# Graph attention from gathered neighbours: edge lists taken from 16-bit words, gathers in groups of three slots

## The chip, the cores and the metric

The kernel runs on one core of a Trainium2 chip. The metric is the device time of one execution in microseconds (us). A core has five engines that run side by side, each in its own order: PE (TensorE, matrix products and transposes), DVE (VectorE, elementwise work, reductions, the eight largest of a row), ACT (ScalarE, activation functions and copies), POOL (GpSimd, here mostly the issuer of indirect DMAs) and SP (SyncE, here only an issuer of DMAs). 16 DMA engines move data between the large memory (HBM) and the core's own memory (SBUF). PE writes to a third memory, PSUM.

## The reference

One graph layer over N = 4096 nodes, D = 512, 8 heads of 64, feed-forward width F = 2048, all in float32. `adj` is a 4096 x 4096 int32 matrix of zeros and ones with about 17 ones a row, `x` the source nodes, `h_target` the target nodes, and `nodemask` is all ones:

```python
hs = layer_norm(x); ht = layer_norm(h_target)
q = (ht @ Wq + bq) / 8; k = hs @ Wk + bk; v = hs @ Wv + bv      # per head
logits = where(adj != 0, q . k, -1e30); probs = softmax(logits)
ht = layer_norm2(ht + (probs @ v) @ Wo + bo)
out = normalise(x + ht + gelu(ht @ W1) @ W2)
```

Only about one logit in 240 is not masked, so the kernel gathers the neighbours' key and value rows rather than computing all logits.

## The kernel before, in words

**Projection (`project`).** `x` and `h_target` are taken 256 rows at a time: normalised (statistics on DVE, the power for 1/sqrt on POOL, scaling on ACT), transposed on PE, multiplied by the weights on PE. For `x` the result is a row of 512 keys and 512 values, stored to the DRAM table `kvd` (4 KB a row; row 0 is zero and serves as padding). For `h_target` it is the query next to the residual row, stored to `tq` (from POOL's queue for the first 20 tiles of 128 target rows, from SP's for the last 12).

**Edge lists (`edges`, L619).** For each tile of 128 target rows the adjacency rows are read in four quarters of 1024 columns. ACT takes the sign (bf16 zeros and ones, with the row's sum as its degree). DVE multiplies by 1 to 128, the position within a segment of 128 columns (L628), and takes the eight largest of each of the eight segments (`max`, L631). The 32 x 8 candidates of a tile get their segment's offset (L634, L637), and five rounds of eight-largest (L641) with four removals (L643) give up to 40 column numbers, row number + 1, into `R`. A count against the degree (L645, and the check in `sort`) raises a flag when a list isn't complete; a flag starts a general path that is not otherwise run.

**Sorting (`sort`, L653).** Target rows are sorted by degree, part A (20 tiles) and part B (12) separately: a one-hot of the degree, small products on PE, a scan on DVE, giving a rank (L690, L692). Then one indirect DMA a tile, issued on POOL, scatters the row's record (list, degree, row number) to its place by rank (L695). After that each sorted tile has a fixed cap of neighbours (`CAPS_A`, `CAPS_B`, from 40 down to 11; 600 slots over all tiles).

**Attention (`attention`, L891).** A slot is one neighbour for each of 128 target rows: one indirect DMA of 128 rows of 4 KB (L794), 512 KB. Slots are handled in groups of S = 4 (L818), each in one of four buffers `kv`. For a group DVE multiplies the keys by the query (L926), sums by head (L930), ACT takes the exponential (L934, or L944 for a tile's first group), and one group later DVE multiplies the values by it (L903, in `values`) and PE transposes and sums them in PSUM (L907). Behind each `values` the gathers of the group three ahead are issued (`issue(k + AHEAD)`). `finish` and the feed-forward (`feed`, L956: L971, gelu on ACT L974, L980) follow for tiles in pairs.

**The order.** Each of these is a Python generator that yields a cost after each portion. `_weave` (L395) always advances the stream with the smallest accumulated cost, each from its own starting value. There are three weaves: projection (all of `x` and the 20 tiles of part A's targets) with the lists of part A; then the rest of the projection with the first sort, the attention of the first three tiles (from 45) and three more lists (from 5); then attention, feed-forward, the remaining lists (at 1.9 times their cost) and the second sort. From the order so written, the language's scheduler makes one fixed order per engine and places the waits; it can move an instruction ahead of others on its engine where its own model finds that engine free. The time of the parts is thus set by queues that do not change at run time: an instruction that waits holds all behind it on its engine, and SP's queue carries adjacency loads, records, weights and `tq` stores one after another.

The lines that set the stages:

```python
_weave((proj, 0), (begin(), 0), (_take(att, early), 45), (_take(ed, 3 * steps), 5))
_weave((att, t0), (chain(feed(g) for g in range(len(GROUPS))), UNIT / 2 + LEAD), (other_lists(), t0))
```

Of the kernel before, what the change touches and what calls it, by code (L numbers as in the profile page):

```python
# [366 lines left out]
BF16 = mybir.dt.bfloat16  # L367

# [60 lines left out]
def adj_resnorm_kernel(  # L429
# [45 lines left out]
    SEG = N // P  # L475
    SQ = SEG // NQ
# [3 lines left out]
    for g in groups:  # L480
        i0 = GROUPS[-1][-1] + 1 if GROUPS else 0
        GROUPS.append(list(range(i0, i0 + len(g))))
    PARTS = ((0, len(CAPS_A)), (len(CAPS_A), len(CAPS_B)))
    S = 4
# [4 lines left out]
    kvd = dram.tile([N + 1, 2 * D], F32, name="kvd")  # L489
# [19 lines left out]
    with tc.tile_pool(name="keep", bufs=1) as keep:  # L509
# [14 lines left out]
        with ExitStack() as late:  # L524
            lp = late.enter_context(tc.tile_pool(name="lists", bufs=1))
            kp = late.enter_context(tc.tile_pool(name="kv", bufs=4))
# [24 lines left out]
            nc.gpsimd.iota(iota_i[:, :SEG], pattern=[[P, SEG]], base=0, channel_multiplier=0)  # L551
            segoff = lp.tile([P, SEG], F32, name="segoff")
            nc.vector.tensor_copy(segoff, iota_i[:, :SEG])
            nc.gpsimd.iota(iota_i, pattern=[[1, P]], base=1, channel_multiplier=0)
            lio = lp.tile([P, P], BF16, name="lio")
            nc.vector.tensor_copy(lio, iota_i)
            bins = lp.tile([P, NB], BF16, name="bins")
            nc.vector.tensor_scalar_add(bins, lio[:, :NB], -1.0)
# [60 lines left out]
            def edges(i):  # L619

                cand = lp.tile([P, SEG, 8], F32, name="cand", bufs=2)
                for h in range(NQ):
                    a = lp.tile([P, QW], I32, name="a", bufs=2)
                    nc.sync.dma_start(a, adj[i * P:(i + 1) * P, h * QW:(h + 1) * QW])
# [3 lines left out]
                    nc.vector.tensor_tensor(sg, sg, lio.unsqueeze(1).to_broadcast([P, SQ, P]),  # L628
                                            ALU.mult)
                    for s in range(SQ):  # L630
                        nc.vector.max(cand[:, h * SQ + s, :], sg[:, s, :])  # L631
                    yield 2.9
                gid = lp.tile([P, SEG, 8], F32, name="gid")
                nc.vector.scalar_tensor_tensor(gid, cand, 0.0,  # L634
                                               segoff.unsqueeze(2).to_broadcast([P, SEG, 8]),
                                               op0=ALU.is_gt, op1=ALU.mult)
                nc.vector.tensor_add(gid, gid, cand)  # L637
# [9 lines left out]
                yield 5.0  # L647
# [5 lines left out]
            def sort(part):  # L653
# [13 lines left out]
                oh = pool.tile([P, SQ, P], BF16, name="sg", bufs=3)  # L667
                oh = oh.rearrange("p s l -> p (s l)")[:, :NB * n].rearrange("p (b i) -> p b i", b=NB)
# [24 lines left out]
                yield 8.0  # L693
# [338 lines left out]
            NA, NBT = PARTS[0][1], PARTS[1][1]  # L1032
# [107 lines left out]
```

## Time and profile before

| | |
|---|---|
| median of 3 runs | 2069.45 us (2065.8 to 2073.72) |
| profiled execution | 2059.0 us, its span 2057.2 us |
| PE busy | 1762.0 us, 86% |
| DVE busy | 1682.1 us, 82% |
| POOL busy | 975.0 us, 47% |
| ACT busy | 747.3 us, 36% |
| DMA | 482.33 MB, 234 GB/s on average |
| gathers of key and value rows | 600 indirect DMAs, 708.7 us of POOL |

The span is the profiled stretch of the one core; the execution's time adds 1.8 us around it. An engine's busy time is a union of its instructions' spans; the instruction lines give a count, the busy time and the mean duration in ns, then the idle time of the engine ahead of them and what ended it. "A <- B" is a wait of A that B ended. Names are the program's own: `L628` is a line of the kernel, `sg<-sg,lio` what is written and read.

### The profile page before, as it was taken

The page shows a single profiled execution, that of the slowest core. Times are in us where ns is not written, and L with a number is a line of the kernel's source. Part 1 is how long each engine was busy: PE and PEld are TensorE (multiplying, and loading weights), DVE is VectorE, ACT ScalarE, POOL GpSimd, SP SyncE. Part 2 cuts the span into 40 slices and gives each one's busy share as a digit, 9 for nine tenths or more (in the row PEclk, how much of TensorE's full clock was granted, in tenths as well). Part 3 has the DMA queues.
Part 4 walks back from the last instruction along what each step waited for, and adds up shares of the span by engine and source line. Part 5 has one row for each costly group of instructions (what it writes and reads, how often), then busy time and mean ns, then how long its engine had stood idle before and what let it go on. Part 6 is the DMA issues. An engine that isn't in the chain of part 4 may idle for free. (4 is left out here: it accounts for less than half of the span.)

```text
span 2057.2 us, 21470 instructions
## 1 busy us (share of the span) xinstructions
PE 1762.0 (86%) x7282; PEld 1142.3 (56%) x7282; DVE 1682.1 (82%) x3022; ACT 747.3 (36%) x1170; POOL 975.0 (47%) x869
## 2 busy tenths in 40 slices
PE   6989888853489999899968998898887899989996
PEld 3444444322366666576646666566565666666664
DVE  5989999558899999999978878797878878887701
ACT  4655555322134543434322333232222243333310
POOL 1023332062445554455676556666655746654301
PEclk9999999986699999999989999999999999999998
DMA  8777776468778687786767777877777768765400
GB/s 275 241 238 242 242 239 213 160 240 321 265 265 282 232 296 240 258 268 224 255 203 263 257 253 240 278 242 269 264 237 249 265 231 271 262 223 198 143 11 23
DMA packets 145391, 482.33 MB, mean 234 GB/s; under 512 B 20293, under 2 KB 20857, under 8 KB 145273
## 3 DMA queue, kind: packets, MB, share of 16 engines
q0 software_dynamic: 100032, 359.45, 51.1%
q1 hardware_dynamic: 39536, 102.53, 15.6%
q10 hardware_dynamic: 5704, 18.89, 2.3%
q8 instruction: 60, 0.98, 0.2%
q14 instruction: 59, 0.48, 0.1%
HBM read 438.07 MB, written 42.73 MB: 234 GB/s over the span
## 5 line engine op out<-in xcount | busy, mean ns | idle before, releaser
L794 POOL DMA_INDIRECT kv<-kvd,rec x600 | 708.7, 1181 | 503.8 <-PE cps L907 287.3
L971 PE MATMUL pf<-h2T,w 128*128 128x256 f32 (+1 forms) x2176 | 476.2, 369 | 2.5 <-ACT h2T L887 2.5
L980 PE MATMUL po<-w,gt 128*128 128x512 f32 x1024 | 470.4, 595 | 0.0
L926 DVE TENSOR_TENSOR kv<-kv,tq 128x2048 f32<-128x2048 f32 (+3 forms) x160 | 344.0, 2151 | 138.5 <-DMA kv<-kvd,rec 120.4
L971 PEld LDWEIGHTS pf<-h2T,w 128*128 128x128 f32 x2176 | 389.3, 192 | 79.5 <-issue 32.7
L907 PE MATMUL cps<-ident,kv 128*128 128x128 f32 x2400 | 323.2, 291 | 121.6 <-DVE kv L903 121.2
L907 PEld LDWEIGHTS cps<-ident,kv 128*128 128x128 f32 x2400 | 294.5, 151 | 191.5 <-DVE kv L903 163.9
L903 DVE TENSOR_TENSOR kv<-kv,p 128x2048 f32<-128x2048 f32 (+3 forms) x160 | 342.4, 2143 | 15.6 <-ACT p L934 15.3
L930 DVE TENSOR_REDUCE lg<-kv 128x32 f32<-128x2048 f32 (+3 forms) x160 | 342.3, 2141 | 0.5
L980 PEld LDWEIGHTS po<-w,gt 128*128 128x128 f32 x1024 | 188.9, 192 | 175.9 <-issue 172.9
L631 DVE MAX8 cand<-sg 128x8 f32<-128x128 bf16 x1024 | 225.9, 276 | 0.1
L609 POOL TENSOR_TENSOR n_rs<-n_ve,mhalf 128x2 f32<-128x2 f32 (+1 forms) x66 | 53.8, 815 | 304.6 <-DVE n_ve L608 260.2
L626 ACT ACTIVATE sg<-a 128x1024 bf16<-128x1024 int32 x128 | 135.1, 1055 | 163.7 <-DVE cand L631 94.8
L974 ACT ACTIVATE gt<-pf 128x512 f32<-128x512 f32 x128 | 76.5, 597 | 253.4 <-PE pf L971 252.3
L934 ACT ACT_TABLE_LOAD x76 | 97.5, 1283 | 194.5 <-DVE lg L930 159.5
L751 PE MATMUL pq<-wk,hT 128*128 128x512 f32 x256 | 121.7, 620 | 17.3 <-ACT row L753 8.3
L751 PE MATMUL pq<-wv,hT 128*128 128x512 f32 x256 | 119.9, 612 | 17.3 <-DVE row L765 10.0
L974 ACT ACT_TABLE_LOAD x103 | 132.1, 1283 | 1.8
L864 PE MATMUL t<-wo,rb 128*128 128x512 f32 x256 | 122.1, 622 | 11.9 <-DVE rb L860 11.9
L934 ACT ACTIVATE p<-lg 128x32 f32<-128x32 f32 (+3 forms) x128 | 25.5, 199 | 276.6 <-DVE lg L930 171.6
L762 PE MATMUL pq<-wq,hT 128*128 128x512 f32 x256 | 121.2, 618 | 3.1 <-DVE row L765 2.6
L628 DVE TENSOR_TENSOR sg<-sg,lio 128x1024 bf16<-128x1024 bf16 x128 | 97.7, 767 | 0.8 <-ACT sg L626 0.8
(119 smaller groups left out, 1408.0 us busy)
## 6 DMA issues: line engine op xcount, KB each, us to landing
a<-in_adj_dram SPq DMA_DIRECT2D x128, 512.0 KB, 5.4
kvd<-row ACTq DMA_DIRECT2D x32, 512.0 KB, 5.5
tq<-row POOLq DMA_DIRECT2D x20, 512.0 KB, 6.1
kv<-kvd,rec POOLq DMA_INDIRECT x600, 5.8
xin<-in_L_gnn_h_target_dram SPq DMA_DIRECT2D x16, 512.0 KB, 4.9
w<-in_L_gnn_W_dram SPq DMA_DIRECT2D x8, 1024.0 KB, 9.6
xin<-in_x_dram SPq DMA_DIRECT2D x15, 512.0 KB, 5.0
tq<-row SPq DMA_DIRECT2D x12, 512.0 KB, 6.6
```

The source lines that it names most:

```text
L626: nc.scalar.activation(sg.rearrange("p s l -> p (s l)"), a, AF.Sign, accum_out=dpart[:, i, h:h + 1])
L631: nc.vector.max(cand[:, h * SQ + s, :], sg[:, s, :])
L751: nc.tensor.matmul(pkv, hT[:, kc, j * P:(j + 1) * P], w[:, kc, :], start=kc == 0, stop=kc == KC - 1)
L794: nc.gpsimd.indirect_dma_start(out=dst, out_offset=None, in_=table[:, :], in_offset=bass.IndirectOffsetOnAxis(ap=idx, axis=0))
L903: nc.vector.tensor_tensor(v4, v4, p[:, j0:j0 + n, :].unsqueeze(3) .to_broadcast([P, n, H, HD]), ALU.mult)
L907: nc.tensor.matmul(cps[:, c, :], kv[:, j, D + c * P:D + (c + 1) * P], ident, is_transpose=True, start=j0 + j == 0 and c == 0, stop=j0 + j ...
L926: nc.vector.tensor_tensor(kv[:, :n, :D], kv[:, :n, :D], tq[:, :D].unsqueeze(1).to_broadcast([P, n, D]), ALU.mult)
L930: nc.vector.tensor_reduce(lg[:, :n, :], kv[:, :n, :D].rearrange("p j (h d) -> p j h d", h=H), AX.X, ALU.add)
L934: nc.scalar.activation(p[:, j0:j0 + n, :], lg[:, :n, :], AF.Exp)
L971: nc.tensor.matmul(pf[:, k, :], w1[(f0 + k) // KC][:, kc, (f0 + k) % KC * P:((f0 + k) % KC + 1) * P], h2T[:, kc, :w], start=kc == 0, stop= ...
L974: nc.scalar.activation(gt, pf, AF.Gelu_apprx_tanh)
L980: nc.tensor.matmul(po[j], gt[:, k, j * P:(j + 1) * P], w2[(f0 + k) // KC][:, (f0 + k) % KC, :], start=False, stop=f0 + k == FC - 1, skip_g ...
```

## The change

1. **Lists from words.** The sign is written as bytes, and pairs of columns are read as one 16-bit word (low byte the even column). The quarter's 512 words are multiplied by 1, 3, 5, ... within a segment, so that each byte that is set becomes an odd position below 256, and the quarter is cut into 5 segments of 102 or 103 words in place of 8 of 128 columns. The eight largest words of a segment are kept: 20 x 8 candidates a tile, each with up to two columns. Two new instructions split them into low and high bytes (`dec`), giving 320 entries where there were 256; the offset, the five rounds and the four removals run over 320. The product goes to a tile of its own (`wd`). The index tables are built once, at the start, by 12 index fills on POOL through one buffer and 16 copies on DVE (before: 2 and 3).
2. **Groups.** S goes from 4 to 3, the `kv` buffers from four to five.
3. **Order.** In the second weave attention starts at 55 (45) and two lists (three) at 60 (5); the remaining ten lists (nine) are in the third. A list's costs in the weave are 4 x 2.0 + 6.0 (4 x 2.9 + 5.0), and the sort's portion ahead of the scatters is given 20.0 (8.0).
4. **Small parts.** The sort's one-hot has a tile of its own instead of one of `sg`'s buffers; the table `kvd` has N + 128 rows, of which the gathers see N + 1 as before.

```diff
-    SEG = N // P
-    SQ = SEG // NQ
+    WQ = QW // 2
+    SQ = 5
+    SEGS = [(s * WQ // SQ, (s + 1) * WQ // SQ) for s in range(SQ)]
+    SEG = NQ * SQ
...
-    S = 4
+    S = 3
...
-    kvd = dram.tile([N + 1, 2 * D], F32, name="kvd")
+    kvd = dram.tile([N + P, 2 * D], F32, name="kvd")
...
-            kp = late.enter_context(tc.tile_pool(name="kv", bufs=4))
+            kp = late.enter_context(tc.tile_pool(name="kv", bufs=5))
...
+            segoff = lp.tile([P, 2, NQ, SQ], F32, name="segoff")
+            for b in range(2):
+                for s, (w0, _) in enumerate(SEGS):
+                    nc.gpsimd.iota(iota_i[:, :NQ], pattern=[[QW, NQ]], base=2 * w0 + b,
+                                   channel_multiplier=0)
+                    nc.vector.tensor_copy(segoff[:, b, :, s], iota_i[:, :NQ])
...
+            nc.gpsimd.iota(iota_i, pattern=[[2, P]], base=1, channel_multiplier=0)
+            lio = lp.tile([P, WQ], U16, name="lio")
+            for w0, w1 in SEGS:
+                nc.vector.tensor_copy(lio[:, w0:w1], iota_i[:, :w1 - w0])
...
-                cand = lp.tile([P, SEG, 8], F32, name="cand", bufs=2)
+                cand = lp.tile([P, SEG, 8], U16, name="cand", bufs=2)
                 for h in range(NQ):
                     a = lp.tile([P, QW], I32, name="a", bufs=2)
                     nc.sync.dma_start(a, adj[i * P:(i + 1) * P, h * QW:(h + 1) * QW])
-                    sg = lp.tile([P, SQ, P], BF16, name="sg", bufs=3)
-                    nc.scalar.activation(sg.rearrange("p s l -> p (s l)"), a, AF.Sign,
-                                         accum_out=dpart[:, i, h:h + 1])
-                    nc.vector.tensor_tensor(sg, sg, lio.unsqueeze(1).to_broadcast([P, SQ, P]),
-                                            ALU.mult)
-                    for s in range(SQ):
-                        nc.vector.max(cand[:, h * SQ + s, :], sg[:, s, :])
-                    yield 2.9
-                gid = lp.tile([P, SEG, 8], F32, name="gid")
-                nc.vector.scalar_tensor_tensor(gid, cand, 0.0,
-                                               segoff.unsqueeze(2).to_broadcast([P, SEG, 8]),
+                    sg = lp.tile([P, QW], U8, name="sg", bufs=3)
+                    nc.scalar.activation(sg, a, AF.Sign, accum_out=dpart[:, i, h:h + 1])
+                    wd = lp.tile([P, WQ], U16, name="wd", bufs=2)
+                    nc.vector.tensor_tensor(wd, sg.bitcast(U16), lio, ALU.mult)
+                    for s, (w0, w1) in enumerate(SEGS):
+                        nc.vector.max(cand[:, h * SQ + s, :], wd[:, w0:w1])
+                    yield 2.0
+                dec = lp.tile([P, 2, SEG, 8], U16, name="dec")
+                nc.vector.tensor_single_scalar(dec[:, 0], cand, 255, op=ALU.bitwise_and)
+                nc.vector.tensor_single_scalar(dec[:, 1], cand, 8, op=ALU.logical_shift_right)
+                gid = lp.tile([P, 2 * SEG, 8], F32, name="gid")
...
-                nc.vector.tensor_add(gid, gid, cand)
+                nc.vector.tensor_add(gid, gid, dec)
...
-                yield 5.0
+                yield 6.0
...
-                oh = pool.tile([P, SQ, P], BF16, name="sg", bufs=3)
...
+                oh = pool.tile([P, NB * NA], BF16, name="oh")
...
-                yield 8.0
+                yield 20.0
...
-                    gather(kvs[k][:, j, :], kvd, recs[i][:, j0 + j:j0 + j + 1])
+                    gather(kvs[k][:, j, :], kvd[0:N + 1, :], recs[i][:, j0 + j:j0 + j + 1])
...
-            _weave((proj, 0), (begin(), 0), (_take(att, early), 45), (_take(ed, 3 * steps), 5))
+            _weave((proj, 0), (begin(), 0), (_take(att, early), 55), (_take(ed, 2 * steps), 60))
```

More of the change, by code (lines that the diff above doesn't have):

```diff
@@ L367 @@
 BF16 = mybir.dt.bfloat16
+U8 = mybir.dt.uint8
+U16 = mybir.dt.uint16
 CAPS_A = (40, 24, 23, 22, 21, 20, 20, 19, 18, 18, 17, 17, 16, 16, 15, 15, 14, 13, 12, 11)
@@ L550, in adj_resnorm_kernel @@
             iota_i = lp.tile([P, P], I32, name="iota_i")
[L551 to L556, printed above, removed]
+            segoff = lp.tile([P, 2, NQ, SQ], F32, name="segoff")
[8 more added lines that the diff above has]
+                nc.vector.tensor_copy(lio[:, w0:w1], iota_i[:, :w1 - w0])
+            nc.gpsimd.iota(iota_i, pattern=[[1, P]], base=0, channel_multiplier=0)
             bins = lp.tile([P, NB], BF16, name="bins")
-            nc.vector.tensor_scalar_add(bins, lio[:, :NB], -1.0)
+            nc.vector.tensor_copy(bins, iota_i[:, :NB])
             lower = lp.tile([P, P], BF16, name="lower")
@@ L1031, in adj_resnorm_kernel @@
             ed = all_edges()
-            NA, NBT = PARTS[0][1], PARTS[1][1]
             steps = NQ + 1
```

7 lines of the change are left out of this document (6 added, 1 removed).

## The prediction

> **What bounds the kernel now.** I read the busy totals first, then busy time by stage, because no engine is the limit throughout. The columns of the second view are the stretch, its length, and busy us (with instructions) of PE, PE's weight loads, DVE, ACT and POOL, then granted clock, DMA share, GB/s.
>
> ```profile
> PE 1762.0 (86%) x7282; PEld 1142.3 (56%) x7282; DVE 1682.1 (82%) x3022; ACT 747.3 (36%) x1170; POOL 975.0 (47%) x869
> ```
> ```profile
> 20.00:380.00 360.00, 325.30 (x872) 149.19 (x871) 327.00 (x1252) 207.01 (x377) 84.60 (x87) 0.98 0.71 229
> 453.00:487.50 34.50, 15.29 (x33) 6.62 (x32) 22.53 (x78) 10.24 (x18) 13.83 (x13) 0.75 1.00 378
> 487.50:575.00 87.50, 39.86 (x219) 33.02 (x220) 75.23 (x82) 10.88 (x25) 35.02 (x32) 0.69 0.76 277
> ...
> 380.00:575.00 195.00, 103.05 (x375) 61.60 (x374) 138.56 (x272) 42.38 (x83) 80.09 (x75) 0.75 0.73 266
> 575.00:1000.00 425.00, 398.75 (x1792) 278.05 (x1792) 414.52 (x760) 176.66 (x261) 227.75 (x196) 0.98 0.75 256
> 1000.00:1110.00 110.00, 88.77 (x401) 62.52 (x400) 90.61 (x89) 27.96 (x41) 77.85 (x65) 0.91 0.72 237
> 1110.00:1930.00 820.00, 734.77 (x3358) 515.00 (x3357) 682.55 (x580) 270.71 (x372) 488.90 (x419) 0.97 0.74 249
> 1930.00:2057.00 127.00, 107.44 (x480) 73.44 (x478) 24.05 (x51) 16.60 (x30) 11.41 (x13) 0.94 0.06 18
> ```
>
> Five stages are seen. In projection with lists (20 to 380) PE and DVE are both at about 90%. Then comes a valley (380 to 575): PE works 103 of 195 us, and in its middle the DMA share is 1.00. From 575 to 1000 attention, feed-forward and the late lists run together, and DVE, 97.5% busy, is the limit. From 1110 to 1930 there are no lists; PE has 90%, DVE 83%, and the two wait for each other and for gathers. The tail is PE's alone. So list work costs time in the first three stages and nothing after 1000.
>
> **Lists.** Instructions on DVE overlap slightly, so I price them from start to start.
>
> ```profile
> 340.72 1.28 DVE L628 TENSOR_TENSOR sg<-sg,lio 128x1024 bf16<-128x1024 bf16 x2
> 341.91 3.19 DVE L631 MAX8 cand<-sg 128x8 f32<-128x128 bf16 x16
> 345.13 0.47 DVE L634 SCALAR_TENSOR_TENSOR gid<-cand,segoff 128x256 f32<-128x256 f32 x1
> ...
> 346.67 0.40 DVE L641 MAX8 R<-gid 128x8 int32<-128x256 f32 x1
> 347.00 0.27 DVE L631 MAX8 cand<-sg 128x8 f32<-128x128 bf16 x1
> ```
> ```profile
> L631 DVE MAX8 cand<-sg 128x8 f32<-128x128 bf16 x1024 | 225.9, 276 | 0.1
> L641 DVE MAX8 R<-gid 128x8 int32<-128x256 f32 x160 | 65.8, 411 | 0.1
> L643 DVE MATCH_REPLACE8 gid<-R,gid 128x256 f32<-128x256 f32 x128 | 52.1, 407 | 0.0
> ```
>
> A product takes (341.91-340.72)/2 = 0.60 us, a segment maximum 3.22/16 = 0.20, a 256-wide maximum 347.00-346.67 = 0.33. The maxima of 128 and 256 differ by 135 ns, so 1.05 ns an element and some 0.065 us fixed. A tile before: 4 x (0.60 + 8 x 0.20) = 8.8, then eleven 256-wide instructions at 0.33 (two for the column numbers, five maxima, four replacements) with about 0.45 for value loads and the count: 4.1. Sum 12.9 us. After: five maxima of about 102 words a quarter at 0.20 - 0.027 = 0.173, and a product of 512 words. No row has a product on words: if its streaming halves it is 0.065 + 0.535/2 = 0.33, if words lose the bf16 rate it stays at 0.60. I take 0.33, since the row nearest to it is of the same two bytes an element. That is 4 x 1.20 = 4.8. The eleven become 320 wide, 0.40 each: 4.4, plus 0.45. Two decodes of 160 words are new: between 0.11 (a quarter of the streaming, 0.065 + 0.042) and 0.23 (all of it, 0.065 + 0.168); I take the middle, 0.17 each. Sum 10.0 us, at worst 4 x (0.60 + 5 x 0.20) + 5.3 = 11.7. **A tile saves 2.9 us** (1.2 at worst): 93 us of DVE over 32 tiles, 58 of them in the first stage. The sign conversion keeps its 1024 elements on ACT; byte output has no row, so I keep its price (ends: 0.2 us either way, hidden while ACT has 207 of 360 us). The product no longer writes over sg, so ACT gets its buffer back after the product, not after eight maxima.
>
> The index tables are ten more round trips between POOL and DVE at the start, ahead of the first norm on POOL:
>
> ```profile
> 11.13 0.23 POOL L554 IOTA iota_i<- 128x128 int32 x1 [8.19 <-DVE cols L574]
> ...
> 11.40 0.29 DVE L556 CAST lio<-iota_i 128x128 bf16<-128x128 int32 x1 [0.26 <-POOL iota_i L554]
> ...
> 16.54 1.01 ACT L741 ACTIVATE hT<-pt,cols 128x256 f32<-128x256 f32 x2
> ...
> 24.43 3.60 PE L751 MATMUL pq<-wk,hT 128*128 128x512 f32 x8
> ```
>
> One trip is 11.69 - 11.13 = 0.56 us, ten 5.6. The first transposed input is ready at 17.55 and used at 24.43, so 6.9 us hide them: cost 0, or 5.6 without that cover.
>
> The Trainium skill, "VectorE: DVE Perf Modes", section on the perf-mode tier table, says that a two-input elementwise instruction on 16-bit data reaches two elements a cycle and no more; the 0.60 us for 1024 elements agrees, and by that rule the product on words, also two bytes wide, would be at the lower of my two ends; at the upper one the lists of the first stage would keep 80 x 0.27 = 22 us more of DVE.
>
> *First stage.* DVE falls to 327 - 58 = 269 of 360 us, and PE's 325 remain. If PE reaches the 93.8% it has from 575 to 1000, the stage is 347 long (gain 13); at 97%, 335 (gain 25). I take **18**, ends 0 (PE held by ACT evictions) and 30.
>
> **The valley.** Next I read it in order of time, with the waits.
>
> ```profile
> 409.38 1.08 POOL L695 DMA_INDIRECT rec<-R,ranki  x1 [36.30 <-DVE ranki L692]
> ...
> 434.41 0.96 POOL L695 DMA_INDIRECT rec<-R,ranki  x1 [0.30 <-issue]
> 435.40 0.73 POOL L609 TENSOR_TENSOR n_rs<-n_ve,mhalf 128x2 f32<-128x2 f32 x1
> ...
> 440.56 1.15 POOL L794 DMA_INDIRECT kv<-kvd,rec  x1 [0.31 <-issue]
> ```
> ```profile
> 469.99 0.69 DVE L765 SCALAR_TENSOR_TENSOR row<-pq,bq 128x512 f32<-128x512 f32 x1 [11.20 <-DMA tq<-row]
> ...
> 487.52 2.27 DVE L926 TENSOR_TENSOR kv<-kv,tq 128x2048 f32<-128x2048 f32 x1
> ```
> ```profile
> 387.44 0.33 ACTq L755 DMA_DIRECT2D kvd<-row  x1
> ```
> ```profile
> kvd<-row ACTq DMA_DIRECT2D x32, 512.0 KB, 5.5
> ```
> ```profile
> 438.94 0.33 SPq L624 DMA_DIRECT2D a<-in_adj_dram  x1
> ...
> 484.92 0.33 SPq L624 DMA_DIRECT2D a<-in_adj_dram  x1
> ```
>
> Sorting, 20 scatters (409 to 435), a norm stuck behind them, first gather at 440.6, yet attention's first DVE instruction only at 487.5: the DMA engines are full, and DVE waits 11.2 us for a row buffer whose store shares SP's queue with adjacency loads. The change starts lists after attention here (60 against 5) and takes two, not three. Between the two quoted loads there are nine, 512 KB each: 4.7 MB, at 378 GB/s 12.5 us. The first four groups are 3, 3, 3 and 2 slots, against 4, 4, 3 and 4: 2.1 MB less, 5.5 us. Together 18. Further, lists cost 14.0 units in the weave, not 16.6: 20 end at 280 of the projection's 336 units (32 portions at 7.8, 20 at 4.3), so DVE is free to sort while PE projects. The gathers need the last k/v store, issued at 387.4 and landing some 5.5 us on, so at most they start at 393, 47 us earlier; at least none, if the planner leaves sorting where it is. I take 15. Against it: two lists (20 us) now lie beside attention, in a stretch where DVE has 12 us idle (75 of 87.5 busy) and which held the end of the third list: a cost of 0 to 8, and I take 3. **Valley: 30**, ends 0 and 62. The weave's new price of 20 behind the sort, on whose result POOL waits 36.3 us, puts more projection ahead of the scatters in the queues; what waits behind them is that norm and the gathers, and I count nothing.
>
> **Late lists.** From 575 to 1000 nine tiles cost 9 x 12.9 = 116 us of DVE; ten will cost 100. The finer groups give back 4 (below). With DVE at 97.5% that is **10**, ends 0 and 20. The second sort's stretch (1000 to 1110) has PE at 81% where the next has 90%, 10 us; its 12 scatters stay, so **3**, ends 0 and 10.
>
> **Groups of three, five buffers.** Summed over the tiles' caps, 160 groups become 210.
>
> ```profile
> L926 DVE TENSOR_TENSOR kv<-kv,tq 128x2048 f32<-128x2048 f32 x139 | 317.6, 2285 | 133.7 <-DMA kv<-kvd,rec 115.6 <-issue 7.5 <-DMA rec<-R,ranki 5.5
> ...
> L926 DVE TENSOR_TENSOR kv<-kv,tq 128x512 f32<-128x512 f32 x6 | 4.1, 682 | 1.2 <-DMA kv<-kvd,rec 1.2
> ```
> ```profile
> POOL kv L794 <- PE cps L907: 110.6, 33, 9.6
> ...
> DVE kv L926 <- DMA kv<-kvd,rec: 91.5, 47, 5.6
> ...
> PE cps L907 <- DVE kv L903: 54.1, 31, 6.8
> ```
>
> The second view is of 1110 to 1930. A slot costs 0.535 us and an instruction 0.14, of which some 0.08 overlaps. Fifty groups with three instructions each: 150 x 0.06 to 0.14 = 9 to 21 us of DVE, mostly where DVE has idle time; its price if it had none is the 21. The gathers stay 600. Before, a gather for group k+3 took the buffer of group k-1 and so waited for PE's transposes of the group just done; with five it takes that of k-2. But the ring holds 15 slots, not 16: less two groups in work, 9 slots are ahead instead of 8. So the 91.5 us of DVE waiting shrink a little, not wholly. At PE's 93.8% the stretch would be 783 us (gain 37); the loss end is the 21 us above. Nearest is no change: **5**.
>
> Sum: 18 + 30 + 10 + 3 + 5 = 66 us off the profiled execution's 2059.0 us (span 2057.2 and 1.8 around it): 1993. The median of the runs is 10.5 us above it, so 2069.45 - 66 = **2003 us**.
>
> **Rivals.** (1) *The ring of five works in full.* For it: 47 of 95 groups wait for a gather. Against: one slot more ahead is little. The 37 us of the long stretch, and half of what the valley has left above my value (32): 2003 - 37 - 16 = 1950.
> (2) *The valley does not move, and words lose the bf16 rate.* For it: sorting and scatters run one after another whatever DVE has free. Then the first stage gives 8, the late lists 4 (ten tiles at 11.7), the valley 8 (half of what the DMA engines are relieved of), the ring its 5: 2069 - 25 = 2044.
> (3) *Slower: exponentials come too late.* ACT changes tables between exponential and gelu:
>
> ```profile
> L934 ACT ACT_TABLE_LOAD x76 | 97.5, 1283 | 194.5 <-DVE lg L930 159.5 <-DVE n_ve L608 8.7 <-DVE degs L838 7.9
> ```
> ```profile
> 1509.07 1.28 ACT L974 ACT_TABLE_LOAD   x1
> ...
> 1510.36 0.60 ACT L974 ACTIVATE gt<-pf 128x512 f32<-128x512 f32 x1
> ```
> ```profile
> DVE kv L903 <- ACT p L934: 15.3, 17, 3.9
> ```
> A group's exponential is hidden by DVE's product and reduction of the next: 2 x 2.2 = 4.4 us with four slots, 2 x 1.67 = 3.3 with three. Behind a gelu it takes 0.6 + 1.28 + 0.2 = 2.1 us, and 3.4 when the gelu's load is still ahead too. So 1.1 us of cover go. It decides from 66/210 = 0.31 us a group; if half of the 210 wait the full 1.1, it costs 115 us: 2118. Against it: today only 17 waits, 15.3 us (the last row, of the long stretch).
>
> The Trainium skill, "ScalarE: Activation LUTs", section "What ACT_TABLE_LOAD costs", adds a drain of 1.38 us to each switch, 2.66 in all. By that the exponential behind a gelu would take 3.5 us, above the new cover, and rival (3) would be likely. The trace has the gelu 10 ns after its load's end, with no such drain, so I leave its chance low.
>
> **Chances.** Forecast 0.56, (1) 0.20, (2) 0.15, (3) 0.09. Half a percent, 10 us, is what a measurement can tell from no change. (2) may end within it (a third of its chance). So faster 0.86, same 0.05, slower 0.09. The range goes from 1935, below rival (1) by the rest of the valley's upper end, to 2060, which takes in nearly all of (2).
>
> **What would show it.** Right: segment maxima near 0.17 us from start to start, 640 of them, products near 0.33; DVE under 80% in the first stage, with PE above 92%; attention's first product before 455 us; POOL's wait for PE's transposes mostly gone, with DVE's wait for gathers still above 60 us in the long stretch. Wrong: scatters still starting 35 us after the last list (valley step), a word product above 0.5 us (list price), or DVE's third instruction waiting for exponentials by more than 60 us (rival 3).

## The result and the profile after

The changed kernel takes **2002.35 us** (median; 1995.04 to 2006.56) against 2068.22 us for the kernel before beside it: a ratio of 0.9674, 95% interval 0.9638 to 0.9710. The forecast was 2003 us. The total is right; the terms it was summed from are not, and most of this text is about that. The traces are single executions: the traced one of the kernel before took 2059.0 us, 9 us less than its median, and the traced one here 2004.54, 2 us more than its median. So the traces show 54 us between the kernels where the medians show 66.

The busy totals of the changed kernel, and its busy time by stage, with the columns as in the prediction (stretch, length, PE, weight loads, DVE, ACT, POOL, granted clock, DMA share, GB/s). The bounds are those of the prediction's stages, moved to where the same work is done now.

```profile
PE 1751.0 (87%) x7282; PEld 1133.6 (57%) x7282; DVE 1599.0 (80%) x2865; ACT 774.0 (39%) x1236; POOL 959.0 (48%) x879
```
```profile
20.00:361.00 341.00, 319.81 (x873) 148.54 (x872) 271.73 (x1052) 205.78 (x378) 83.77 (x87) 0.98 0.72 242
361.00:549.00 188.00, 108.36 (x430) 66.49 (x429) 123.58 (x220) 42.87 (x83) 84.61 (x76) 0.78 0.75 267
549.00:972.00 423.00, 405.31 (x1788) 278.53 (x1788) 409.85 (x757) 191.14 (x287) 233.66 (x203) 0.96 0.76 263
972.00:1070.00 98.00, 79.29 (x347) 54.89 (x346) 75.44 (x78) 28.80 (x44) 59.14 (x55) 0.88 0.72 247
1070.00:1879.00 809.00, 732.66 (x3398) 514.53 (x3396) 692.06 (x680) 283.34 (x409) 480.63 (x421) 0.97 0.75 254
```

DVE lost 83 us of work (1682.1 before) and left the first stage, where it has 272 of 341 us. The stages after it have nearly the shape they had.

**The list step** shows in its group by line (busy us and mean ns) and in a stretch of DVE's timeline (start, duration):

```profile
L644 DVE MAX8 cand<-wd 128x8 uint16<-128x102 uint16 (+1 forms) x640 | 130.8, 251 | 0.8
```
```profile
461.35 0.74 DVE L642 TENSOR_TENSOR wd<-sg,lio 128x512 uint16<-128x512 uint16 x2
462.01 1.76 DVE L644 MAX8 cand<-wd 128x8 uint16<-128x102 uint16 x10
463.69 1.21 DVE L944 TENSOR_TENSOR kv<-kv,tq 128x1024 f32<-128x1024 f32 x1
```

A word product takes (462.01 - 461.35)/2 = 0.33 us from start to start, a segment maximum 1.68/10 = 0.168, and there are 640 of them, as forecast.

**The valley** in order of time. Rows of several engines are put together.

```profile
309.97 1.16 DVE L687 TENSOR_TENSOR oh<-b,bins 128x960 bf16<-128x960 bf16 x1
...
372.37 0.37 PE L697 MATMUL t<-oh,ones_bf 128*128 128x480 bf16 x1
...
390.42 1.31 POOL L713 DMA_INDIRECT rec<-R,ranki  x1 [38.20 <-DVE ranki L710]
...
423.13 0.97 POOL L812 DMA_INDIRECT kv<-kvd,rec  x1 [0.30 <-issue]
...
437.17 1.76 DVE L944 TENSOR_TENSOR kv<-kv,tq 128x1536 f32<-128x1536 f32 x1 [4.84 <-DMA kv<-kvd,rec]
```

DVE has the sort's one-hot table ready at 311.1, but PE's first product on it runs at 372.37: it stands 61 us behind projection products in PE's queue (before: 17 us, from 374.97 to 391.79). The scatters start at 390.42, 19.0 us earlier than before (409.38). From the first gather to attention's first product it now takes 437.17 - 423.13 = 14.0 us, where it took 487.52 - 440.56 = 47.0. So the first product comes 50 us earlier. Then this follows on SP's queue, DVE and ACT:

```profile
473.00 6.65 SPq L1071 DMA_DIRECT2D w<-in_L_gnn_W_dram  x1
479.76 8.72 SPq L637 DMA_DIRECT2D a<-in_adj_dram  x2
497.72 1.06 ACT L640 ACTIVATE sg<-a 128x1024 uint8<-128x1024 int32 x1 [22.55 <-DMA a<-in_adj_dram]
...
498.89 1.56 SPq L637 DMA_DIRECT2D a<-in_adj_dram  x2
...
502.35 0.20 ACT L952 ACTIVATE p<-lg 128x24 f32<-128x24 f32 x1
502.59 1.75 DVE L921 TENSOR_TENSOR kv<-kv,p 128x1536 f32<-128x1536 f32 x1 [19.72 <-ACT p L952]
```

The next adjacency load goes out only at 479.76, behind six weight loads whose issue has SP from 459.39 to 479.65. Two loads are issued by 488.48; the next two follow at 498.89, when the first sign has set its load's buffer free (there are two). ACT waits 22.55 us with that sign for the first load; the exponential is queued behind the signs, and DVE waits 19.72 us for the exponential.

How far attention is can be read by counting PE's transposes (four to a slot) up to a time. The first rows are of the kernel before, the second of the changed one (columns: stretch, length, PE and weight-load busy us with counts, clock, DMA share, GB/s).

```profile
0.00:602.00 602.00, 27.27 (x162) 24.56 (x162) 0.90 0.72 244
0.00:1025.00 1025.00, 110.71 (x799) 100.80 (x800) 0.93 0.74 250
0.00:1126.00 1126.00, 133.40 (x964) 121.47 (x964) 0.93 0.73 248
0.00:1948.00 1948.00, 322.57 (x2396) 294.14 (x2397) 0.95 0.73 246
```
```profile
0.00:576.00 576.00, 26.31 (x160) 22.80 (x161) 0.91 0.73 252
0.00:997.00 997.00, 111.67 (x796) 98.62 (x797) 0.93 0.74 256
0.00:1085.00 1085.00, 131.99 (x959) 116.92 (x960) 0.93 0.75 258
0.00:1897.00 1897.00, 319.64 (x2395) 285.84 (x2396) 0.95 0.74 253
```

The same count is reached 26, 28, 41 and 51 us earlier, and the span ends 54.4 us earlier (2002.8 for 2057.2). By stage, with a second trace beside it: run B below turned out to have the same instructions in the same order on every engine.

| stage | forecast | trace | run B's trace |
|---|---|---|---|
| first stage (start of the scatters) | 18 | 19 | 7 |
| valley, to slot 40 | 30 | 7 | 8 |
| late lists, slots 40 to 200 | 10 | 2 | 6 |
| second sort, slots 200 to 240 | 3 | 13 | 12 |
| long stretch, slots 240 to 600 | 5 | 10 | 7 |
| tail | 0 | 3 | 3 |

So the first stage's gain differs by 12 us between two executions of the same instructions, and that of the late lists by 4. Smaller differences than these, between single traces, say nothing.

Whole-span waits of the changed kernel (total us, times, longest):

```profile
POOL kv L812 <- PE cps L925: 250.1, 94, 16.1
...
DVE kv L944 <- DMA kv<-kvd,rec: 118.1, 48, 7.1
...
DVE kv L921 <- ACT p L952: 33.0, 13, 19.7
```

### The profile page after: what moved, and what is told of

It reads as the page before. It is cut to its first block, busy times and chain, and to the rows that moved or that the text cites. A ratio compares the mean times of both kernels' runs of the same rounds, so it can differ in the third digit from the quotient of the medians.

```text
span 2002.8 us, 21520 instructions
## 1 busy us (share of the span) xinstructions
PE 1751.0 (87%) x7282; PEld 1133.6 (57%) x7282; DVE 1599.0 (80%) x2865; ACT 774.0 (39%) x1236; POOL 959.0 (48%) x879
## 5 line engine op out<-in xcount | busy, mean ns | idle before, releaser
L812 POOL DMA_INDIRECT kv<-kvd,rec x600 | 687.6, 1146 | 464.6 <-PE cps L925 250.1
L989 PE MATMUL pf<-h2T,w 128*128 128x256 f32 (+1 forms) x2176 | 485.9, 374 | 3.6 <-ACT h2T L905 3.6
L944 DVE TENSOR_TENSOR kv<-kv,tq 128x1536 f32<-128x1536 f32 (+2 forms) x210 | 351.2, 1674 | 130.5 <-DMA kv<-kvd,rec 118.1
L925 PEld LDWEIGHTS cps<-ident,kv 128*128 128x128 f32 x2400 | 286.4, 147 | 169.3 <-DVE kv L921 127.3
L921 DVE TENSOR_TENSOR kv<-kv,p 128x1536 f32<-128x1536 f32 (+2 forms) x210 | 349.3, 1666 | 33.2 <-ACT p L952 33.0
L948 DVE TENSOR_REDUCE lg<-kv 128x24 f32<-128x1536 f32 (+2 forms) x210 | 349.3, 1666 | 0.5
L640 ACT ACTIVATE sg<-a 128x1024 uint8<-128x1024 int32 x128 | 135.0, 1055 | 146.5 <-DMA a<-in_adj_dram 90.4
L952 ACT ACTIVATE p<-lg 128x24 f32<-128x24 f32 (+2 forms) x178 | 34.3, 193 | 320.3 <-DVE lg L948 161.4
L644 DVE MAX8 cand<-wd 128x8 uint16<-128x102 uint16 (+1 forms) x640 | 130.8, 251 | 0.8
L780 PEld LDWEIGHTS pq<-wq,hT 128*128 128x128 f32 x256 | 51.0, 206 | 78.8 <-issue 60.1
```

Of the source, the lines that this page charges most:

```text
L780: nc.tensor.matmul(pq, hT[:, kc, j * P:(j + 1) * P], wq[:, kc, :], start=kc == 0, stop=kc == KC - 1)
L812: nc.gpsimd.indirect_dma_start(out=dst, out_offset=None, in_=table[:, :], in_offset=bass.IndirectOffsetOnAxis(ap=idx, axis=0))
L921: nc.vector.tensor_tensor(v4, v4, p[:, j0:j0 + n, :].unsqueeze(3) .to_broadcast([P, n, H, HD]), ALU.mult)
L925: nc.tensor.matmul(cps[:, c, :], kv[:, j, D + c * P:D + (c + 1) * P], ident, is_transpose=True, start=j0 + j == 0 and c == 0, stop=j0 + j ...
L944: nc.vector.tensor_tensor(kv[:, :n, :D], kv[:, :n, :D], tq[:, :D].unsqueeze(1).to_broadcast([P, n, D]), ALU.mult)
L948: nc.vector.tensor_reduce(lg[:, :n, :], kv[:, :n, :D].rearrange("p j (h d) -> p j h d", h=H), AX.X, ALU.add)
```

## The experiments

All times are medians of five rounds or more beside the kernel before, which had 2069.82 us in the first four runs, 2071.75 in the next four and 2071.24 in the last four. Ratios are to that.

### The parts one by one

**Words alone.** The new lists, with their costs in the weave and the small parts, but neither groups nor order:

```diff
 changed kernel
-    S = 3
+    S = 4
-    tile_pool(name="kv", bufs=5)
+    tile_pool(name="kv", bufs=4)
-    (_take(att, early), 55), (_take(ed, 2 * steps), 60)
+    (_take(att, early), 45), (_take(ed, 3 * steps), 5)
-    yield 20.0      (after the sort)
+    yield 8.0
```


> The word lists alone (with their new weave costs of 14.0 units a tile), groups of four in four buffers, the order of before. Theory A, the prediction's steps: the first stage gives 18 us, the valley about 5 (three lists there are 2.9 us cheaper each), the late lists, DVE-bound at 97.5%, nine times 2.9 us = 26 of which some 20 are seen: 2068 - 43 = about 2025. Theory B, as the two traces line up by milestones (the stretch with late lists took as long after as before): only the first stage pays, 2068 - 19 = about 2049. In both a product on 512 words takes 0.33 us from start to start.

2033.28 us, ratio 0.9827 (0.9788 to 0.9866): 36 us, between the two theories (43 and 19). DVE's busy total falls from 1682.1 to 1600.1 us, 82 us where the list price said 93. But the gain does not lie where it was forecast. This trace reaches slot 40 at 574 us, 28 before the kernel before, slot 200 at 1010, only 15 before it, and slot 240 at 1103, 23 before it. The stretch of the late lists grew from 423 to 436 us, though DVE had 391.79 us of work in it in place of 411.10. So less list work did not shorten that stretch by itself; what held it there is not settled.

**Groups alone.**

```diff
 kernel before
-    S = 4
+    S = 3
-    tile_pool(name="kv", bufs=4)
+    tile_pool(name="kv", bufs=5)
```


> The kernel before with groups of three in five buffers and nothing else. Theory A (prediction): about 5 us faster, 2063, with DVE's wait for gathers a little shorter. Rival, the ring of five works in full: 2040 or below, POOL's and DVE's waits for buffers and gathers mostly gone. Rival, exponentials too late: slower than 2078, with DVE's third instruction waiting for ACT far above 15 us.

2003.10 us, ratio 0.9677 (0.9643 to 0.9710): 67 us, as much as the whole change, where the prediction had 5, and well past the 2040 of the rival. Counts of transposes in this run:

```profile
0.00:590.00 590.00, 25.01 (x157) 21.33 (x157) 0.92 0.73 247
0.00:1113.00 1113.00, 133.00 (x964) 116.35 (x964) 0.94 0.74 251
0.00:1528.00 1528.00, 235.52 (x1761) 207.89 (x1762) 0.95 0.76 258
0.00:1909.00 1909.00, 315.70 (x2400) 282.05 (x2400) 0.95 0.74 252
```

The kernel before reaches the first two counts at 602 and 1126, the third at 1577 and the last at 1948:

```profile
0.00:1577.00 1577.00, 240.98 (x1757) 218.36 (x1757) 0.94 0.74 250
```

So the groups win 12 us before slot 40, nothing more to slot 240, then 36 us in a stretch of 200 slots without any list work, and give 10 of these back to slot 600: the long stretch gains 26. The span ends 50.5 us earlier (2006.7 for 2057.2); the rest of the 67 is the distance of the two traced executions from their medians.

**Order alone.**

```diff
 kernel before
-    (_take(att, early), 45), (_take(ed, 3 * steps), 5)
+    (_take(att, early), 55), (_take(ed, 2 * steps), 60)
-    yield 8.0      (after the sort)
+    yield 20.0
```


> The kernel before with the new order alone: attention from 55, two lists from 60, the sort's portion at 20. Theory A (prediction's valley step): attention's first product some 20 to 35 us earlier, the valley 15 us shorter, a tenth late list of 12.9 us given back: about 2065. Theory B (order is what moves the valley, the late stage hides the tenth list): 2040.

2074.43 us, ratio 1.0025 (1.0004 to 1.0047): no gain, against both theories (2065 and 2040), and a loss too small to tell from no change. Attention does start earlier, as theory A asked: its first product runs at 466.80, 21 us before the kernel before's, and 15.8 us behind the first gather (47.0 before). But slot 40 comes at 602, no earlier than before, after a stall like that of the changed kernel: DVE waits 16.74 us for one exponential.

**Words and order without the groups.**

```diff
 changed kernel
-    S = 3
+    S = 4
-    tile_pool(name="kv", bufs=5)
+    tile_pool(name="kv", bufs=4)
```


> The changed kernel with groups of four in four buffers again. Theory A (groups are worth 5 us): 2007. Theory B (from the milestones: from the second sort on the changed kernel gained another 10 to 20 us, by the finer ring): 2020.

2048.89 us, ratio 0.9896 (0.9857 to 0.9935), slower than both theories: without the groups 47 us of the changed kernel's gain are gone. Against words alone the order costs 16 us. This trace has the same stall, 20.0 us at the longest, where words alone has 2.1.

**Words and groups in the old order.**

```diff
 changed kernel
-    (_take(att, early), 55), (_take(ed, 2 * steps), 60)
+    (_take(att, early), 45), (_take(ed, 3 * steps), 5)
-    yield 20.0      (after the sort)
+    yield 8.0
```


> The changed kernel with the old order: word lists in 20 segments, groups of 3 and five buffers, but attention from 45, three lists from 5 and a sort portion of 8. Theory A (the parts add up: groups alone took 66 us off, words alone 36): 2069 - 66 - 36 = 1967 us. Theory B (groups and words take away waits of the same stretch, so that the second of them finds little left): within 10 us of the groups alone and of the whole change, 1995 to 2010 us. Theory C (the new order is worth some 15 us once the words are there, as between the words alone at 2033 and words with order, which came out at 2049, it was not): then this kernel would be below the whole change by about 15 us, 1987 us.

1977.08 us, ratio 0.9540 (0.9514 to 0.9566). Words (36) and groups (67) nearly add up: 95 of 103 us. The new order takes 25 of them back in the changed kernel.

### What of the order costs

Three edits make the order. Two runs put one back each; a third moves the remaining lists.

```diff
 changed kernel, run A: the lists' place
-    (_take(ed, 2 * steps), 60)
+    (_take(ed, 3 * steps), 5)
```


> The changed kernel with three lists from 5 as before, in place of two from 60; attention from 55 and the sort's portion of 20 stay. Against the changed kernel (2002 us) and words with groups in the old order (1977 us). Theory A (the list that is moved out of the stretch before 500 us, where DVE is mostly idle, into the stretch that DVE fills is what the new order costs): 1977 to 1987 us. Theory B (the place of the first attention portions or of the sort is): 1997 us or more.

```diff
 changed kernel, run B: the sort's portion
-    yield 20.0
+    yield 8.0
```


> The changed kernel with the portion behind the sort back at 8 in place of 20; lists and attention stay in the new order. Theory A (the 20 pushes scatters and gathers behind more projection and later pushes the second sort behind more attention): 1977 to 1990 us. Theory B (the portion matters little): 1998 to 2006 us.

```diff
 changed kernel, run C: the lists after the sort
-    (other_lists(), t0)
+    (other_lists(), t0 + 20)
```


> The changed kernel with the remaining lists' work woven in 20 us of planned time later, behind the loads of the last weights. It tests the stretch at 482 to 502 us, in which DVE waited 19.7 us for an exponential that stood behind a sign on ACT, and that sign for an adjacency load behind weight loads on SP. Theory A (a stall of that kind sets the end by its length): 2002 - 18 = 1984 us. Theory B (the stall is moved to another place or made good by the long stretch, in which the buffers run ahead again): 1998 to 2006 us. Theory C (the lists that come later push the second sort late, and the second half's gathers with it): 2010 us or more.

A takes 1975.46 us (ratio 0.9552, 0.9522 to 0.9582), the same as the whole old order; B takes 2005.98 (0.9687, 0.9660 to 0.9715), C 1999.25 (0.9660, 0.9632 to 0.9687), both the same as the changed kernel. So it is the lists' place alone. The other two edits hardly reach the chip: the fixed order that the scheduler makes for B is that of the changed kernel, instruction for instruction on every engine, and that for A differs from the whole old order in some twenty places out of 12,500 instructions. B is thus a second measurement of the changed kernel, 4 us from the first, and no test of the portion of 20 beyond this: it changes nothing. C was meant to take the 20 us stall away and didn't: its longest wait of that kind is still 20.0 us, so the theories on the stall were not told apart by it.

A tells more. SP's queue behind the late weights, and the counts of transposes in run A:

```profile
478.93 2.50 SPq L1071 DMA_DIRECT2D w<-in_L_gnn_W_dram  x1
543.73 14.75 SPq L637 DMA_DIRECT2D a<-in_adj_dram  x4
```
```profile
0.00:571.00 571.00, 25.88 (x163) 22.70 (x164) 0.93 0.75 258
0.00:982.00 982.00, 108.10 (x800) 96.17 (x801) 0.94 0.76 261
0.00:1076.00 1076.00, 128.41 (x964) 114.85 (x964) 0.95 0.75 259
0.00:1868.00 1868.00, 311.87 (x2400) 280.65 (x2400) 0.96 0.75 257
```

With three lists from 5, the adjacency loads are out before the weights, the next come at 543.73, and no exponential stands behind a sign that waits for them: the longest wait is 2.9 us. All five kernels with the lists' new place have a wait of 16.7 to 20.0 us there, and none with the old place has one above 3.9. Run A is 5 us ahead of the changed kernel at slot 40, 15 at slot 200, 9 at slot 240, 29 at slot 600. The first 15 have two likely places: the stall, which uses up the early start of attention, and one list tile of about 10 us that the changed kernel leaves to the stretch in which DVE is 97% busy (409.85 of 423 us). The second sort gives 6 back, and 20 arise after slot 240, where no list work is left in either kernel. There the changed kernel's DVE waits more for gathers (34.8 us against 18.3 from 1150 to 1500); why the lists' place reaches so far is not settled by these runs.

### Why the groups gain

**Four buffers of three.**

```diff
 kernel before
-    S = 4
+    S = 3
```


> The kernel before with groups of 3 slots, still four buffers and gathers three groups ahead. Theory A (what the groups brought is the fifth buffer: a gather asked three groups ahead goes into a buffer set free one group earlier, so POOL no longer waits for the transposes of the group just before): with four buffers the wait is back and 12 slots are in flight in place of 16, so 2065 to 2090 us. Theory B (what they brought is the smaller group: shorter bursts of transposes and products, so that DVE and PE wait shorter for each other): 2003 to 2025 us, as with five buffers.

2115.28 us, ratio 1.0220 (1.0191 to 1.0248), slower than both theories allowed. Smaller groups alone lose 44 us; the fifth buffer turns that into a gain of 67. What a fifth buffer does for groups of four no run shows.

**Five buffers, all of them asked for ahead.**

```diff
 kernel before
-    S = 4
+    S = 3
-    tile_pool(name="kv", bufs=4)
+    tile_pool(name="kv", bufs=5)
-    AHEAD = 3
+    AHEAD = 4
```


> The kernel before with groups of 3, five buffers, and gathers asked four groups ahead in place of three: 15 slots in the ring, all of them asked for, and each gather again waits for the buffer of the group just before. Theory A (the slack of one buffer between asking and setting free is what brought the gain): it is gone, 2050 to 2075 us. Theory B (small groups are what brought it): 2003 us or a few us to either side. Theory C (more slots asked ahead would hide the gathers better, since DVE still waited 85 us for them with three ahead): below 1995 us.

2001.72 us, ratio 0.9658 (0.9631 to 0.9684): as with three ahead. The traces say why: between 1150 and 1500 us the first gather into a buffer starts 1.3 us on average after the buffer's last transposes here, 1.4 us with three ahead, and 1.2 in the kernel before. So a gather follows the freeing of its buffer just as closely, whatever group it was asked behind. The slack between asking and setting free, which the prediction describes, does not arise, so it is not the cause.

What is, one can follow in the timeline of the kernel before (rows of several engines together). The code takes the buffers in turn, so every fourth group has the same one. One use of a buffer, from its first gather to its next one (the rows at 1300.32, 1302.80 and 1310.87 are of the group behind it):

```profile
1290.27 0.95 POOL L794 DMA_INDIRECT kv<-kvd,rec  x1 [0.30 <-issue]
...
1295.32 0.94 POOL L794 DMA_INDIRECT kv<-kvd,rec  x1 [0.30 <-issue]
...
1300.32 0.93 POOL L794 DMA_INDIRECT kv<-kvd,rec  x1 [0.63 <-PE cps L907]
...
1302.00 2.25 DVE L926 TENSOR_TENSOR kv<-kv,tq 128x2048 f32<-128x2048 f32 x1
1302.80 2.27 POOL L794 DMA_INDIRECT kv<-kvd,rec  x1 [0.30 <-issue]
...
1310.87 2.29 DVE L926 TENSOR_TENSOR kv<-kv,tq 128x2048 f32<-128x2048 f32 x1 [4.30 <-DMA kv<-kvd,rec]
...
1319.67 2.28 DVE L903 TENSOR_TENSOR kv<-kv,p 128x2048 f32<-128x2048 f32 x1
...
1322.01 1.97 PE L907 MATMUL cps<-ident,kv 128*128 128x128 f32 x16 [0.32 <-DVE kv L903]
...
1324.60 0.94 POOL L794 DMA_INDIRECT kv<-kvd,rec  x1 [0.30 <-issue]
```

Four gathers are issued in 5.0 us, 6.7 us later the key product starts, 17.7 us later the values product of the same group (two other groups' key products stand between), then 4.3 us to the end of the transposes and 0.6 to the next use: 34.3 us in all, for four buffers 8.6 us a group. The count of key products in 350 us without lists, here for the kernel before, says 350/41 = 8.5 us a group:

```profile
1150.00:1500.00 350.00, 88.83 (x41) 0.97 0.76 256
```

That the two agree proves nothing yet: buffers that are taken in turn come round after n groups, whatever sets the pace. That the ring holds the work back shows in two waits of the next group. Its first gather (1300.32) waits for PE's transposes to set a buffer free, and its key product (1310.87) finds DVE idle for 4.30 us, until its last gather lands. Such waits of DVE are 39.5 us of these 350. With four buffers, two groups' time of a cycle is the wait for the values product, so n groups take (issue + landing + transposes + reuse) + 2 groups, and **a group takes that bracket divided by n - 2**. The same count for four buffers of 3, five of 3, and the last run below, each a trace of its own:

```profile
1150.00:1500.00 350.00, 88.45 (x52) 0.96 0.73 246
```
```profile
1150.00:1500.00 350.00, 98.31 (x58) 0.98 0.82 278
```
```profile
1150.00:1500.00 350.00, 105.57 (x89) 0.96 0.83 285
```

The bracket below is the mean over the groups that start in this stretch, taken in each trace from rows like those of the example; the waits are DVE's for gathers in these 350 us:

| buffers x slots | bracket us | rule, us a group | count, us a group | waits us | time us |
|---|---|---|---|---|---|
| 4 x 4 (before) | 17.4 | 8.7 | 8.5 | 39.5 | 2070 |
| 4 x 3 | 14.5 | 7.2 | 6.7 | 49.8 | 2115 |
| 5 x 3 | 16.1 | 5.4 | 6.0 | 24.4 | 2003 |
| 6 x 2 | 14.7 | 3.7 | 4.2 | 30.8 | 2032 |
| 7 x 2, words, old order | 17.4 | 3.5 | 3.9 | 8.0 | 1951 |

The waits fall in the order of the times, and so does the rule's time for one slot: 2.4 us with 4 x 3, then 2.2, 1.8 and 1.8, and 1.7 with 7 x 2. The bracket comes out of the same trace as the count, so the table is an account and not a forecast. With four buffers the rule gives what is seen, within half a microsecond. With more, the values product follows its key product by 2.2 to 2.7 groups in place of 2, and a group takes longer than the rule says. The rule says where the gain has its source, not its full size: from 5.4 to 6.0 us it is engines, or waits among them.

**Six buffers of two**, the same 12 slots as four of three:

```diff
 kernel before
-    S = 4
+    S = 2
-    tile_pool(name="kv", bufs=4)
+    tile_pool(name="kv", bufs=6)
-    AHEAD = 3
+    AHEAD = 5
```


> The kernel before with groups of 2 slots, six buffers and gathers five groups ahead: 12 slots in the ring, as in the run with groups of 3 in four buffers (2115 us). Theory A (ring rule: a buffer is held for its gathers' issue and landing, then for two whole groups until its values product, then for its transposes; so with n buffers a group takes (issue + landing + transposes) / (n - 2). From the traces between 1150 and 1500 us that gives 17.4 / 2 = 8.7 us for four buffers of 4, 14.5 / 2 = 7.2 for four of 3, 16.1 / 3 = 5.4 for five of 3, against 8.5, 6.7 and 6.0 seen; for six buffers of 2 it gives about 13 / 4 = 3.2 us, less than the 3.6 us that DVE needs for such a group, so the ring no longer binds): the gathers' waits nearly go, DVE gets 147 groups more with 0.06 to 0.14 us for each of three instructions, 26 to 62 us, and the time is 1990 to 2030 us. Theory B (what counts is the slots in flight: 12 are as slow as the other 12): 2100 us or more.

2032.06 us, ratio 0.9821 (0.9793 to 0.9850), 83 us below the other 12 slots and 2 us above the range that the ring rule gave. The number of slots in the ring alone is not what counts. The bracket was put at about 13 us and came to 14.7. That the gathers' waits nearly go did not come true: DVE still waits 83.1 us for them over the span (120.4 in the kernel before).

**Seven buffers of two, with words and the old order:**

```diff
 changed kernel, old order
-    S = 3
+    S = 2
-    tile_pool(name="kv", bufs=5)
+    tile_pool(name="kv", bufs=7)
-    AHEAD = 3
+    AHEAD = 5
```


> Words and groups with the old order (1977 us), but groups of 2 in seven buffers, gathers five groups ahead. Theory A (the ring rule: (about 13) / 5 = 2.6 us a group, not binding): of the 81 us that DVE waited for gathers most go, against 97 groups more, 17 to 41 us of DVE: 1955 to 1985 us. Theory B (a group's exponential has too little cover, two instructions of 1.2 us against 3.4 us behind a gelu): DVE's wait for exponentials grows by 0.3 us or more for each of 307 groups: 2050 us or more.

**1950.58 us**, ratio 0.9428 (0.9400 to 0.9456): 52 us below the changed kernel, the fastest run of this case, and 4 us below the range given. The busy totals and the waits that both theories name:

```profile
PE 1747.6 (90%) x7282; PEld 1131.5 (58%) x7282; DVE 1626.9 (83%) x3156; ACT 802.5 (41%) x1341; POOL 892.4 (46%) x879
```
```profile
DVE kv L944 <- DMA kv<-kvd,rec: 44.0, 37, 3.7
...
DVE kv L921 <- ACT p L952: 21.6, 35, 2.3
```

The wait for gathers falls to 44.0 us (118.1 in the changed kernel), and the exponentials, with still smaller groups, cost 21.6 us in 35 waits. DVE has 25.5 us more to do than with groups of 3 (1626.9 against 1601.4 in the run with words and groups), and it pays.

## Why the prediction was right, and where it was not

**The total is right by errors that cancel.** Groups are worth 67 us alone and stood at 5; valley and late lists stood at 40 and came to 9 in one trace of the changed kernel and 14 in the other; the order, which was to bring the valley's gain, costs 25. That these make 66 together is luck.

**Lists: the price was right, nearly.** Product 0.33 us, maximum 0.168, as forecast; DVE's total falls by 82 us, 2.6 us a tile, where 2.9 was forecast. Words alone give 36 us against the 31 that the prediction has for first stage, late lists and second sort, but this agreement is in part chance, since the late lists' stretch grew in that run. The Trainium skill, "VectorE: DVE Perf Modes", section on the perf-mode tier table, gives two-byte operands of a two-input instruction two elements a cycle; the trace agrees, with 0.33 us for 512 words against 0.60 us for 1024 bf16 elements, 1.6 and 1.7 elements a ns. The first stage's term (18) is 19 in one trace and 7 in the other, so its step is neither confirmed nor refuted to better than some 10 us. DVE has 271.73/341 = 79.7% there, PE 319.81/341 = 93.8%, as the signs asked.

**Valley: wrong in two steps.** "DVE is free to sort while PE projects" is true, and useless: the sort also needs PE, and its products (L697) stand behind the projection in PE's queue until 372.37. I had counted the portion of 20 as putting more projection ahead of the scatters; as run B shows, it does not change the order of a single instruction. The named sign of failure came true: the table for the sort is ready at 311.1, the scatters start 79 us later. The other step, fewer transfers ahead of the gathers, was right and more than I gave it: the first product comes 33 us sooner after the first gather (18 forecast, with the groups' smaller start in it). Order alone brings 31 of these, and groups alone none: 47.0 us again, from 440.13 to 487.18. But it is lost again within 70 us. What I priced at 3 us, "two lists now lie beside attention", is the 19.72 us stall: I counted DVE's time for these lists and not the queue that their loads and signs share with weights and exponentials.

**Late lists: the limit was wrong.** The step was that DVE, 97.5% busy, sets the length of that stretch, so that less list work shortens it. Words alone took 19 us of DVE's work out of it, and it grew by 13 us, with DVE at 391.79/436 = 90%. The changed kernel, with its ten lists, gains 2 us there (6 in run B) against 10 forecast. Run A, with the same words and groups and nine lists, takes 571 to 982 in place of 602 to 1025 and gains 12, where the same sum gives 9 x 2.9 - 4 = 22. So the words pay in that stretch only together with the groups, and less than DVE's time says.

**Groups: the term that was mis-sized.** The step that failed is "less two groups in work, 9 slots are ahead instead of 8. So the 91.5 us of DVE waiting shrink a little". The count of slots is right, but a buffer's whole cycle held the work back, and a smaller group shortens that cycle too: its issue, its transposes and the two groups that it waits. The reason given for the little that it allowed, that with five buffers a gather takes the buffer of one group earlier and no longer waits for the transposes, did not come about either: it starts 1.4 us behind them, where it was 1.2. By the rule above a slot falls from 17.4/8 = 2.2 us to 16.1/9 = 1.8 in the ring. I took DVE's waits for gathers as all there was to win, and little of them as to be had. The 21 us that I gave as the price of 50 more groups are there: DVE's three group instructions take 20.6 us more in the run with groups alone.

**The rivals.** (1), the ring in full, names the right mechanism for the gain of groups alone: my 37 us for the long stretch are 26 there. In the changed kernel the long stretch gains only 10 (7 in run B), and 30 in run A. Its total of 1950 needed a valley that kept its gain. (2) fell with the 0.33 us. (3), exponentials too late, showed itself once and for another reason: not a smaller group's cover, but a sign ahead of the exponential that waited for a load. Apart from that wait the kernel has 33.0 - 19.7 = 13.3 us, less than the 15.3 before.

**The other signs.** POOL's wait for PE's transposes was to be mostly gone and is not: it is 250.1 us against 287.3. Attention's first product came at 437 (before 455 asked). DVE's wait for gathers in the long stretch stayed at 87.6 us (above 60 asked).

## What to carry to other kernels

For a ring of gather buffers, write down one buffer's whole cycle from the trace, from its first gather to its next one. If the gather waits for the buffer and the engine that uses it waits for the gather, the ring holds the work back, and smaller groups in more buffers can be worth their extra instructions; smaller groups in as many buffers were not. Before work is moved into another stretch, follow each of its instructions through every queue that it enters, loads and conversions too, and see which instruction of the critical work is next in that queue. When a sum comes out right, time each part alone before any of its terms is believed, and see in the instruction order of each run that the edit has changed anything.

## What was not expected of the hardware

The issue of one 1 MB weight load held SP for 6.65 us, and that of the two 512 KB loads behind it for 8.72, where an adjacency load takes SP 0.33 us at 438.94 in the kernel before. In the same stretch the DMA engines are 96% busy, and PE, busy for 10.44 of 50 us, is granted half its clock:

```profile
450.00:500.00 50.00, 10.44 (x44) 8.84 (x44) 32.87 (x65) 5.26 (x12) 20.28 (x15) 0.50 0.96 362
```

A gather takes POOL 0.94 us in most rows, but 2.27 in one of the rows of the ring's example (at 1302.80), which adds 1.3 us to the issue of its group.
